# A gated recurrence on one core: groups of three steps of h instead of four, with the products of x made for one pair and for two pairs in turn

## The chip, the cores and the metric

The kernel runs on one core of one Trainium2 chip. The metric is the device time of the whole program in microseconds (us), lower is better. Three runs of the kernel before took 3062.22, 3062.46 and 3062.75 us, so the time before is their median, 3062.46 us.

## The reference

Two layers are computed one after the other on x, which holds 64 sequences of 256 steps of 1024 numbers, all in float32:

```python
xW = jnp.einsum('ntd,dh->nth', x, Wx) + b
def step(prev_h, xw):
    next_h = jnp.tanh(prev_h @ Wh + xw)
    return (next_h, next_h)
...
x = x + h_t
h = jax.nn.silu(q_pool @ W1.T + b1)
gate = jax.nn.sigmoid(h @ W2.T + b2)[:, None, :]
...
a = a * gate
...
return v + a
```

The first layer is a recurrence: h of each step needs h of the step before, times the 1024 x 1024 matrix Wh, plus the row of x Wx of this step, and a tanh. The second layer takes the sequence apart into sums and differences, multiplies every one of them by the same gate of 1024 numbers for each sequence, and puts them together again. Because all are multiplied by one gate, the result is x times (1 + gate); with the residual, x times (2 + gate). The kernel uses that: it makes one `factor` = 2 + gate and multiplies.

## The kernel before, in words

Work comes in **steps** t (0 to 255) and in **pairs** i = t // 2 (0 to 127), since S = 2 steps of x are loaded together as one 512 KB slab. Two kinds of product fill TensorE.

- **A step of h** (`h Wh`, the loop from line 716 on) is done by Strassen's scheme: seven products of blocks instead of eight, each by `strassen_product` (line 192, its matmul is line 197). A product is 16 calls on column strips of 32, and shows in the trace as 32 matmuls and 32 weight loads, so a step is 224 matmuls and 224 weight loads. Between the products ScalarE copies partial sums and does tanh (`tanh`, `put_next`), and VectorE adds, transposes h (`transpose`) and makes the sides of the next step (`strassen_sides`).
- **x Wx of a pair** (class `XWork`, matmul at line 276) is done in three passes of split numbers: `mixed` from x2, then `main` from x1 and from x0, 48 matmuls of 128 x 512 in all (`whole`, line 333). VectorE splits x into `high` (L123), `x2` (`difference`, L305) and `x1` (`low`, L300); ScalarE makes `x0` (`cast`, L311). ScalarE takes `mixed` out of PSUM (`take_mixed`, L321), GpSimd adds the bias (L322), VectorE adds `main` to it (`finish_half`, L376). The tile `sum` then goes to DRAM (`store`, L386) and comes back in another order as the `xw` of two steps (`reload`, L399, eight transfers).

Steps 0 to 11 (up to ALONE = 12) set up the gate and interleave both kinds at a finer grain; the change doesn't touch that part. From step 12 on the order of TensorE, VectorE, ScalarE, GpSimd and SyncE is the order of the program text (`tc.manual_schedule`), so what is written first is queued first on each engine.

In that part the kernel works in **groups** of M = 4 steps of h, and after each group it calls `beside_x(t, mark)`, the **gap**: x Wx of two pairs, named `one` and `two`, while a third (`three`) is split for the next gap. Gaps are at t = 11, 15, ..., 251: 61 of them, and the last has one pair only. PSUM is shared: the banks `main0` and `main1` of x Wx also hold two of the seven products of a step (`m5`, `m7`).

What else a gap does, in program order on SP, the queue that issues the transfers: store `sum` of the pair left from the gap before (held back until the copy `mark` in the last step of the group, by `not_ahead_of`), load x of pair i + 4, reload of the pair just stored, store y of a finished pair, load x of pair i + 5, store and reload of `one`, store y of the second finished pair. GpSimd multiplies the four finished steps by the factor (`scale`, L501). `kept_step` does one of ten early half-finished steps in every second gap (a load, a multiplication on GpSimd, a store). A slab of x is free again once its `store_y` has landed; there are six slabs.

One ScalarE instruction lies inside the group: in its first step, after the first copy, `coming.cast()` makes x0 of the pair that opens the next gap:

```python
if t % M == 0 and coming is not None:
    coming.cast()
```

The tiles `xw` of steps lie in three buffers of a pool; every fourth step (`self.i * S % M + s == M - 1`) uses a fourth buffer, `h0T`.

## Time and profile before

| what | value |
|---|---|
| median of three runs | 3062.46 us |
| the profiled execution's own time | 3049.05 us |
| its span, first to last instruction | 3047.2 us |
| granted TensorE clock, mean | 1.000 |
| matmuls of x Wx (L276) | 4064 + 2032, 389 and 394 ns each |
| matmuls of h Wh (L197), one of its seven groups | 7808 or 8160, 273 ns each |
| VectorE, ScalarE, GpSimd busy | 59%, 28%, 27% of the span |
| transfers of data (queue q1) | 163856 packets, 290.81 MB |
| instruction fetches (queue q8) | 501 packets, 8.21 MB |

The profiled execution took 3049.05 us by its own time, 1.85 us more than its span and 13.4 us less than the median of the runs. The sums of the prediction are made inside the profiled span.

The views are read like this. The timeline lists the instructions of one engine in order of time: start, duration, engine, line, operation, output <- inputs, tile shape, output shape, count; in brackets stands idle time ahead of it. The table of windows gives, for each stretch, its length, then each engine's busy time and count, the granted clock and the share and rate of the DMA engines. The chain of waits follows the last instruction back to what released it. "issue" is time in which an engine waited for nothing that the profile shows.

### The profile page before, as it was taken

To read this page: it belongs to the slowest core of one execution; us is meant where nothing else is said; L and a number is where in the kernel's file an instruction comes from. 1 tells how busy PE (TensorE), PEld (TensorE's weight loads), DVE (VectorE), ACT (ScalarE), POOL (GpSimd) and SP (SyncE) were. 2 spreads that over 40 slices of the span, in tenths; PEclk is the share of its full clock that TensorE was granted. 3 is DMA by queue.
4 is the path that set the end of the run, shared out by engine and by line. 5 is a ranking of instruction groups with operands and counts; after the bars stand their busy time and mean duration, and the time that the engine had idled before them with its cause. 6 is when DMAs were issued, how large, how long until landed. Compare 5 with 4: busy or idle time off the path is not lost.

```text
span 3047.2 us, 141801 instructions
## 1 busy us (share of the span) xinstructions
PE 3029.6 (99%) x63862; PEld 2716.6 (89%) x63862; DVE 1791.4 (59%) x4928; ACT 866.9 (28%) x2641; POOL 808.3 (27%) x521
## 2 busy tenths in 40 slices
PE   9999999999999999999999999999999999999999
PEld 6888898988989989899899898988988989989898
DVE  8555655656656556565565555655656556556565
ACT  3222222322223222222232222222322223222222
POOL 2222222232232231222222222222132222231221
PEclk9999999999999999999999999999999999999999
DMA  7323323233232232322322313223222232232322
GB/s 264 121 83 111 97 88 113 80 104 106 80 120 86 92 119 67 109 88 84 113 77 95 107 65 113 87 85 113 73 99 94 77 113 80 92 112 68 104 92 76
DMA packets 164606, 300.41 MB, mean 99 GB/s; under 512 B 44192, under 2 KB 110496, under 8 KB 164000
## 3 DMA queue, kind: packets, MB, share of 16 engines
q1 hardware_dynamic: 163856, 290.81, 28.2%
q8 instruction: 501, 8.21, 1.1%
q14 instruction: 105, 0.86, 0.1%
q10 hardware_dynamic: 144, 0.52, 0.1%
HBM read 154.93 MB, written 136.31 MB: 96 GB/s over the span
## 4 chain that ended last, share of the span: by engine, by line
PE 99%; issue 0%; POOL 0%; DMA 0%; DVE 0%; SPq 0%; ACT 0%; DVEq 0%
PE main L276 30%; PE acc L197 22%; PE mixed L276 16%; PE m_h L197 14%; PE main_h L197 14%; PE m L197 1%; PE acc L214 0%; PE gate_ps L214 0%; POOL sum L322 0%; DMA wx<-wx 0%; PE acc_raw L214 0%; DVE x L300 0%; SPq L413 0%; ACT sum L321 0%; SPq L119 0%
## 5 line engine op out<-in xcount | busy, mean ns | idle before, releaser
L276 PE MATMUL main<-wx,x 128*128 128x512 f32 x4064 | 945.8, 389 | 0.6 <-DVE x L300 0.6
L276 PEld LDWEIGHTS main<-wx,x 128*128 128x128 f32 x4064 | 762.0, 188 | 161.5 <-issue 2.6
L322 POOL TENSOR_TENSOR sum<-sum,b_row 128x512 f32<-128x512 f32 x254 | 409.9, 1626 | 1119.0 <-ACT sum L321 1109.4
L501 POOL TENSOR_TENSOR x<-x,factor 128x512 f32<-128x512 f32 x242 | 368.2, 1531 | 1007.0 <-issue 561.4
L276 PE MATMUL mixed<-wx,x 128*128 128x512 f32 x2032 | 491.7, 394 | 0.0
L276 PEld LDWEIGHTS mixed<-wx,x 128*128 128x128 f32 x2032 | 376.3, 188 | 89.6 <-issue 12.9
L729 ACT ACTIVATE h<-h 128x128 f32<-128x128 f32 x976 | 275.6, 306 | 568.5 <-DVE h L753 396.7
L300 DVE TENSOR_TENSOR x<-x,x_high 128x1024 fp32r<-128x1024 f32 x127 | 176.9, 1393 | 269.8 <-PE main L276 269.7
L733 DVE STREAM_TRANSPOSE hT<-h 128x128 f32<-128x128 f32 x972 | 297.8, 306 | 38.4 <-ACT h L729 38.3
L376 DVE SCALAR_TENSOR_TENSOR sum<-main,sum 128x512 f32<-128x512 f32 x254 | 175.4, 691 | 203.1 <-PE main L276 181.4
L197 PE MATMUL acc<-wh,s 128*32 128x128 f32 x8160 | 282.6, 273 | 1.3 <-issue 1.0
L197 PE MATMUL acc<-wh,hT 128*32 128x128 f32 x8160 | 279.5, 273 | 1.6 <-issue 1.3
L197 PE MATMUL acc<-t,hT 128*32 128x128 f32 x8160 | 277.8, 273 | 2.2 <-issue 2.0
L197 PE MATMUL m_h<-t,s 128*32 128x128 f32 x7808 | 269.5, 273 | 1.1 <-issue 0.9
L197 PE MATMUL main_h<-wh,s 128*32 128x128 f32 x7808 | 269.7, 273 | 0.8 <-issue 0.6
L197 PE MATMUL main_h<-t,s 128*32 128x128 f32 x7808 | 269.2, 273 | 1.2 <-issue 0.8
L197 PE MATMUL m_h<-wh,hT 128*32 128x128 f32 x7808 | 266.8, 273 | 2.0 <-issue 1.7
L305 DVE SCALAR_TENSOR_TENSOR x<-x_high,x 128x1024 fp32r<-128x1024 f32 x127 | 174.5, 1374 | 155.3 <-PE mixed L276 155.2
L321 ACT ACTIVATE sum<-mixed 128x512 f32<-128x512 f32 x254 | 144.8, 598 | 364.7 <-DMA sum_d<-sum 221.2
L197 PEld LDWEIGHTS acc<-wh,s 128*32 128x32 f32 x8160 | 238.0, 110 | 4.3 <-issue 4.1
L197 PEld LDWEIGHTS m_h<-wh,hT 128*32 128x32 f32 x7808 | 217.8, 110 | 26.3 <-issue 25.9
L614 ACT COPY acc<-xw 128x128 f32<-128x128 f32 x732 | 185.2, 264 | 191.6 <-DVE y L769 102.4
(81 smaller groups left out, 2793.5 us busy)
## 6 DMA issues: line engine op xcount, KB each, us to landing
x<-xT SPq DMA_DIRECT2D x127, 512.0 KB, 4.4
sum_d<-sum SPq DMA_DIRECT2D x127, 512.0 KB, 2.9
xw<-sum_d SPq DMA_DIRECT2D x1016, 64.0 KB, 2.0
yT<-x SPq DMA_DIRECT2D x122, 512.0 KB, 3.5
wh<-wh SPq DMA_DIRECT2D x8, 512.0 KB, 10.7
w<-w1T SPq DMA_DIRECT2D x8, 512.0 KB, 8.6
w<-w2T SPq DMA_DIRECT2D x8, 512.0 KB, 5.0
wx<-wx SPq DMA_DIRECT2D x7, 512.0 KB, 8.6
```

Source lines behind the costliest of these rows:

```text
L197: nc.tensor.matmul(out=out[q * R : (q + 1) * R], lhsT=a[:, k * R : (k + 1) * R], rhs=wh_s.sides[i][k][:, q], start=first and k == 0, stop= ...
L276: nc.tensor.matmul(out=acc[h], lhsT=v[:, k * P : (k + 1) * P], rhs=wx_s[k][which][:, h * HALF : (h + 1) * HALF], start=start and k == 0, s ...
L300: nc.vector.tensor_sub(self.x1, x, self.high)
L305: nc.vector.scalar_tensor_tensor(out=self.x2, in0=self.high, scalar=1.0 + DOWN, in1=pairs[i], op0=ALU.mult, op1=ALU.subtract)
L321: nc.scalar.activation(s, self.mixed[h], AF.Copy, scale=-1.0)
L322: nc.gpsimd.tensor_add(s, s, b_row[:, h * HALF : (h + 1) * HALF])
L376: nc.vector.scalar_tensor_tensor(out=v, in0=self.main[h], scalar=1.0 + DOWN, in1=v, op0=ALU.mult, op1=ALU.add)
L501: nc.gpsimd.tensor_mul(of_step(x, s), of_step(x, s), blocks(factor))
L614: nc.scalar.copy(part, xws[t // S][t % S][:, j])
L729: nc.scalar.activation(quad(h, j), quad(h, j), AF.Tanh)
L733: nc.vector.transpose(quad(hT, j), quad(h, j))
```

## The change

M becomes 3. From step 12 on there are groups of three steps (the last has four), 81 gaps at t = 11, 14, ..., 251, and x Wx of two pairs and of one pair stand in the gaps in turn. `beside_x` gets the pair left over (`later`), the pair that is split (`coming`), the steps to multiply (`scaled`) and the last step of the next group (`end`), and decides by `many` whether it does a second pair. In a gap of one pair the pair's `sum` is not stored at once: it becomes `later`, whose store waits for the `mark` of the next group, as that of `two` did. Loads of x and stores of y are now counted off (`load_next`, `store_done`) instead of being written for fixed pairs; a pair of x is loaded at most five ahead of the last stored one. `kept_step` counts gaps instead of steps. The place of the fourth `xw` buffer is written with 4 instead of M.

```diff
@@ -69,7 +69,7 @@
 E = F // 2
 KB = B // 2
 S = 2
-M = 4
+M = 3
 NP = T // S
 HALF = 512
 HIGH = -(1 << 12)
@@ -390,7 +390,7 @@
             xw = []
             for s in range(S):
                 name = f"xw{self.i * S + s}"
-                if late and self.i * S % M + s == M - 1:
+                if late and (self.i * S + s) % 4 == 3:
 
                     t = const.tile([P, 4, E], F32, tag="h0T", name=name)
                 else:
@@ -629,73 +629,99 @@
     def store_y(i: int) -> None:
         nc.sync.dma_start(out=yT[i], in_=pairs.pop(i))
 
-    def beside_x(t: int, mark):
-
-        i = t // S
-        steps = [(i - 1, 0), (i - 1, 1), (i, 0), (i, 1)] if mark else [(i, 1)]
-        if mark:
+    groups = [M] * ((T - ALONE) // M - 1) + [(T - ALONE) % M + M]
+    done = [ALONE // S - 1]
+    loaded = [i + 3]
+
+    def load_next() -> None:
+
+        k = loaded[0] + 1
+        if k > done[0] + 5:
+            return
+        if k < NP:
+            load_x(k)
+        elif k == NP:
+            ends.append(slab("ends"))
+            nc.sync.dma_start(out=ends[0][:, :W], in_=xN)
+        loaded[0] = k
+
+    def store_done(t: int) -> None:
+
+        while (done[0] + 1) * S <= t + 1:
+            store_y(done[0])
+            done[0] += 1
+
+    def beside_x(t: int, later, coming, scaled: list, end: int, mark):
+
+
+        if later:
             d, dma = later.store()
             not_ahead_of(dma, mark)
-        if i + 4 < NP:
-            load_x(i + 4)
-        if mark:
-            xws[i + 1] = later.reload(d, True)
-        one = coming
-        one.whole()
+        fresh = loaded[0] < NP
+        load_next()
+        if later:
+            xws[later.i] = later.reload(d, True)
+        now, half = coming, len(scaled) // 2
+        many = now.i + 1 < NP and now.i <= end // S
+        now.whole()
         residual(t, hT)
-        for j, r in steps[:2]:
-            scale(pairs[j], r)
-        if mark:
-            store_y(i - 1)
-        if i + 5 < NP:
-            load_x(i + 5)
-        elif i + 4 < NP:
-            ends.append(slab("ends"))
-            nc.sync.dma_start(out=ends[0][:, :W], in_=xN)
-        one.take_mixed()
+        for r in scaled[: half + 1]:
+            scale(pairs[r // S], r % S)
+        if many:
+            store_done(scaled[half])
+            load_next()
+        now.take_mixed()
         if mark:
             accs[:] = [put_part(t + 1, j) for j in range(3)]
-        two = three = None
-        if i + 3 < NP:
-            two = XWork(i + 3)
-            two.difference()
-            two.low()
-        else:
+
+        def prepare():
+            if now.i + 1 == NP:
+                return None
+            nxt = XWork(now.i + 1)
+            nxt.difference()
+            nxt.low()
+            return nxt
+
+        nxt = prepare()
+        if not fresh and not factors:
 
             x_n, factor_n = ends[0][:, :W], ends[0][:, W:]
             nc.vector.transpose(factor_n, factor)
             nc.vector.tensor_mul(x_n, x_n, factor_n)
...
+            factors.append(factor_n)
+        now.finish_half(0)
+        now.finish_half(1)
+        for r in scaled[half + 1 :]:
+            scale(pairs[r // S], r % S)
+        kept_step()
+        if now.i <= end // S:
+            d, _ = now.store()
+            store_done(t)
+            xws[now.i] = now.reload(d, True)
+            if many:
+                now = nxt
+                now.cast()
+                now.whole()
+                now.take_mixed()
+                nxt = prepare()
+                now.finish_half(0)
+                now.finish_half(1)
+                return now, nxt
+            return None, nxt
+        store_done(t)
+        return now, nxt
 
     again = []
 
-    def kept_step(t: int) -> None:
-
-        n, odd = divmod(t // M - ALONE // M, 2)
+    def kept_step() -> None:
+
+        n, odd = divmod(gaps[0], 2)
+        gaps[0] += 1
 
         def at(v, n: int):
             return v[n // S].rearrange("p (b s n) -> p s b n", b=B, s=S)[:, n % S]
 
-        if not 0 <= n <= S * len(kept):
+        if n > S * len(kept):
             return
         if odd and again:
             v = again[0][:].rearrange("p (b g m) -> p g b m", b=B, g=G)
@@ -710,13 +736,14 @@
                 nc.sync.dma_start(out=v, in_=at(kept, n))
 
     accs = [put_part(ALONE, j) for j in range(3)]
-    coming, later, ends = later, None, []
-    coming.cast()
-    later, coming = beside_x(t, None)
+    ends, factors, gaps = [], [], [0]
+    later.cast()
+    later, coming = beside_x(t, None, later, [t], t + groups[0], None)
+    first = ALONE
     for t in range(ALONE, T):
         i, s = divmod(t, S)
         final = t == T - 1
-        last_of_group = t % M == M - 1
+        last_of_group = t == first + groups[0] - 1
         xw = xws[i][s]
         m16, m5, m7 = (bank(tag, f"{tag}_h{t}")[:, :E] for tag in ("m16", "main0", "main1"))
         y = sums.tile([P, 4, E], F32, tag="y", name=f"y{t}")
@@ -745,7 +772,7 @@
 
         strassen_product(m16, sides[1], 1, True)
         nc.scalar.copy(y[:, 0], m16)
-        if t % M == 0 and coming is not None:
+        if t == first and coming is not None:
             coming.cast()
         strassen_product(accs[2], sides[4], 4)
         strassen_product(accs[0], sides[2], 2)
@@ -757,10 +784,10 @@
         if final:
             times_factor(slice(0, E))
             plus_x(slice(0, E))
-        elif t > T - M:
+        elif t > T - 4:
 
             v = x_step(t - 1)
-            nc.vector.tensor_mul(v, v, blocks(factor)) if t < T - 1 else None
+            nc.vector.tensor_mul(v, v, blocks(factor))
             store_y(i - 1) if t == T - S else None
         put_next(0)
         strassen_product(m16, sides[6], 6)
@@ -796,7 +823,10 @@
             nc.vector.tensor_mul(blocks(last[:, :W]), x_step(t), blocks(factor))
             nc.sync.dma_start(out=yT[i][:, :W], in_=last[:, :W])
         elif last_of_group:
-            later, coming = beside_x(t, mark)
+            group = range(first, t + 1)
+            first = t + 1
+            del groups[0]
+            later, coming = beside_x(t, later, coming, list(group), t + groups[0], mark)
         else:
             residual(t, hT)
 
```

## The prediction, made before the change was run

> **What bounds the kernel now.** I read the page first, then who waited for whom on TensorE (PE), then PE's own timeline, cut into steps.

> ```profile
> span 3047.2 us, 141801 instructions
> ...
> PE 3029.6 (99%) x63862; PEld 2716.6 (89%) x63862; DVE 1791.4 (59%) x4928; ACT 866.9 (28%) x2641; POOL 808.3 (27%) x521
> ...
> PE 99%; issue 0%; POOL 0%; DMA 0%; DVE 0%; SPq 0%; ACT 0%; DVEq 0%
> ```

> The chain that ended last is PE alone. So a gain must come from PE's own stream: fewer instructions, or fewer holes between them. The waits of PE show which holes there are:

> ```profile
> PE acc L197 <- issue: 4.3, 11, 0.7
> PE m_h L197 <- issue: 2.6, 8, 0.4
> PE main_h L197 <- issue: 1.5, 5, 0.4
> PE main L276 <- DVE x L300: 0.6, 1, 0.6
> ```

> After the set-up no other engine and no transfer ever makes PE wait; there is only "issue", 8.4 us, all inside products of h. But a slowed stream need not show as idle. So I took from PE's timeline the start of every step and every gap, and measured stretch by stretch. A group without losses (four steps, then the gap), then the worst group, then the last gap, the only one with a single pair:

> ```profile
> core 0: us, PE busy (x), PEclk, DMA share, GB/s
> 2605.84:2611.98 6.14, 6.14 (x226) 1.00 0.02 4
> 2611.98:2618.09 6.11, 6.11 (x233) 1.00 0.02 5
> 2618.09:2624.20 6.11, 6.11 (x232) 1.00 0.02 5
> 2624.20:2630.43 6.23, 6.23 (x233) 1.00 0.09 36
> 2630.43:2652.41 21.98, 21.98 (x100) 1.00 0.54 183
> ...
> 1992.56:1998.69 6.13, 6.13 (x225) 1.00 0.02 5
> 1998.69:2004.81 6.12, 6.12 (x233) 1.00 0.01 4
> 2004.81:2012.25 7.44, 6.61 (x230) 1.00 0.02 4
> 2012.25:2018.93 6.68, 6.62 (x228) 1.00 0.10 36
> ...
> 3005.46:3016.57 11.11, 11.11 (x51) 1.00 0.35 116
> ```

> The first number after a stretch is its length. Full groups take 24.59 us (203.47 to 228.06, and the one above), the worst takes 26.37. Over the 60 full groups I summed what lies above 24.59 us: **28.9 us**, in 41 groups 0.1 us or more. By place: the first two steps lose 0.05 us in all 60 groups together, the third 6.9 us, the fourth 22.0 us. Something that is full at the start of a group runs out in its third or fourth step, and a gap restores it. That is the quantity the change acts on.

> [...] of the 22 holes after 300 us, every one ends 2.3 to 3.0 us after an instruction fetch, so holes come once per block at a fixed place in it. A step has 448 PE instructions (224 matmuls, 224 weight loads), so a lossless step uses a block each 6.115 x 256 / 448 = 3.49 us, while fetches in the group from 1004 us come at 1007, 1011, 1014, 1018, 1022 and 1026, some 3.8 us apart. [...] The trace has it end between 12 and 24 us. [...] h uses strips of 32 columns and x the whole array. [...]

> **Part 1: twenty more gaps.** Gaps at t = 11, 15, ..., 251 are 61; at 11, 14, ..., 251 they are 81. The instructions on PE stay the same: 244 steps, 121 pairs. Each gap costs PE two changes of kind. On the h side: four inner steps of 6.1145 us (7 products of 0.8735) would be 24.46, the lossless group has 24.59, so 0.13. On the x side: two pairs take 21.98, one pair 11.11, so a pair is 10.87 and the gap's fixed cost 0.24. Together 0.37 us, on the path: 20 x 0.37 = **+7.4 us**. Bounds 0.3 and 0.45 us: +6 to +9.

> **Part 2: no fourth step.** 80 of 81 groups end after the third step. The fourth steps' 22.0 us go. The third step's loss is met 80 times, not 60: 6.9 x 80 / 60 = 9.3 us. The last group keeps four steps, before and after. So 28.9 becomes 9.3: **-19.6 us**. The place of block borders in a group wanders in both versions (a group and its gap before are no multiple of 256), so the mean over all groups is the right row; its scatter (0.27 us a group) makes 9.3 into 4 to 18.

> **Part 3: does half a gap refill the reserve?** Counting 256 per fetch and subtracting the PE instructions started, I get the lead of the fetching side up to a constant. It is mostly -20 to -80 late in groups that lost time; of all fetches that fall later than 3.2 us into a gap, in any gap, each finds it at 83 to 106. A short gap is 11.1 us, so I cost this at nothing; without that cover it is the rival below.

> **Part 4: what else lies in a short gap.** VectorE: the end of the step (to 2.0 us after the gap's start), residual 0.7, `high` 0.7, x2 after the mixed pass (1.4), x1 after the x1 pass (1.3), then the two `finish_half`. Of the second pair of a present gap (ending 1051.36):

> ```profile
> 1049.71 0.69 DVE L376 SCALAR_TENSOR_TENSOR sum<-main,sum 128x512 f32<-128x512 f32 x1 [0.64 <-PE main L276]
> 1051.54 0.69 DVE L376 SCALAR_TENSOR_TENSOR sum<-main,sum 128x512 f32<-128x512 f32 x1 [1.14 <-PE main L276]
> 1054.32 0.29 DVE L753 TENSOR_TENSOR h<-acc,y 128x128 f32<-128x128 f32 x1 [2.10 <-PE acc L197]
> ```

> Bank `main0` is free at 1050.4 and `main1` at 1052.2, while `m5` and `m7` first write them 2.6 and 4.4 us after 1051.36: over 3 us of slack, the same in a short gap. ScalarE's `take_mixed` waits for the store of `sum` as now; `put_part` after a short gap takes steps whose xw came a gap earlier, so it waits less. Casts in a first step rise from 61 to 81 at 1.05 us; the first step lost nothing with one in it. GpSimd multiplies two of three steps inside the group, now two of four; 1.5 us each on an engine 27% busy. SP: the same 121 stores and reloads, loads and y stores; a short gap holds one store (2.9 us to land), one load of x, eight reloads (4.6 us to issue) and one y store, some 12 us of queue with `kept_step`; a tail may fall in the first steps of h, where transfers of up to 0.4 MB already lie in several groups without loss. The next store of `sum` waits for `mark` 16 us later. Nothing: 0 us; if this fails by 0.3 us in 40 short gaps, +12.

> **Sum.** -19.6 + 7.4 = -12.2 us of a 3047.2 us span, so 3035.0 there. The runs' median is 13.4 us above the profiled execution's own 3049.05; I take the difference over as it is: 3062.5 - 12.2 = **3050.3 us**, 0.4% faster.

> **Rivals.** (a) *Short gaps refill too little* (slower). For: in the last group, after the only short gap, the third step ended 0.72 us late, six times the mean of 0.12. Against: it is one group, seven of 60 after long gaps lost over 0.5 by there, and the lead above. If 40 groups after short gaps lose 0.72 each: 28.8 + 40 x 0.117 + 7.4 - 28.9 = +12.0, so 3074.5 us. It decides from 0.57 us a group, where the sum passes +6. (b) *The loss is only moved*: supply sets the pace on average, or a wait appears in short gaps, 0.3 us each; -12.2 + 12 = 0, 3062.5 us. For: the lead falls in every group, also without losses. Against: long stretches of PE in gaps use few instructions. (c) *Luck of the block borders is better* and third steps lose half: 4.7 instead of 9.3, so -17, 3045.7 us; counted with the forecast.

> **How the numbers follow.** Forecast with (c): 0.69, from 3043 (loss 4, gaps +6) to 3060 (loss 18, gaps +9). (b) 0.18; (a) 0.13. A measurement of this kernel can tell about 0.2%, 6 us, from no change. Faster, below 3056.4: 0.65 of the forecast and 0.05 of (b), 0.70; same 0.18; slower 0.12. The range leaves out (a) and the far ends: 3043 to 3064.

> **What would show it.** After: span near 3035; groups of three take 18.5 us, losing about 0.12 on average, all in the third step; gaps 11.1 and 22.0 us in turn; PE "issue" well under 8 us. Wrong if groups after short gaps lose more than those after long ones (rival a), or if PE waits for another engine at the start of a group (b).

## The result and the profile after

The changed kernel took 3055.27 us, median of 15 runs (3049.82 to 3056.55); the kernel before took 3062.22 us beside it, median of 15 (3054.38 to 3066.93). The ratio is 0.9976 with a 95% interval of 0.9968 to 0.9984: 7 us or 0.24% faster, where I had forecast 12.2 us. The time lies in the range that was given; but that range, 3043 to 3064 us, also held the time of no change at all, so the interval of the ratio, which leaves out 1, says more.

The profiles seem to say the opposite. The profiled execution of the kernel before had taken 3049.05 us, less than any of the 15 runs; the one after took 3056.46 us by its own time, among the highest of its runs. The page of after begins:

```profile
span 3054.6 us, 141755 instructions
...
PE 3039.8 (100%) x63862; PEld 2716.7 (89%) x63862; DVE 1796.3 (59%) x4928; ACT 864.0 (28%) x2641; POOL 772.3 (25%) x521
...
PE 99%; issue 0%; POOL 0%; DMA 0%; DVE 0%; SPq 0%; ACT 0%; DVEq 0%
```

The number of matmuls is the same and PE still bounds all; its busy time rose by 10 us because a stretch in which matmuls come late counts mostly as busy: of the last two steps of the worst group below, 6.89 and 8.14 us long, 6.58 and 6.83 us count so, against 6.12 and 6.22 in the group without loss. So the two pages can't be subtracted: they are executions in which the same stream ran at different speeds. The waits of PE after (in total, times, longest):

```profile
PE acc L197 <- issue: 4.0, 9, 0.7
PE main_h L197 <- issue: 2.1, 7, 0.3
PE m_h L197 <- issue: 0.6, 2, 0.3
PE main L276 <- DVE x L300: 0.4, 1, 0.4
```

"issue" is 6.7 us, against 8.4 before. No wait for another engine came in its place: the 0.4 us for VectorE lie in the set-up. The table of windows of after, PE alone (stretch, its length, PE's busy time and count, granted clock, DMA share and GB/s): a group of three without loss, a long gap, a group that lost 0.35 us, a short gap, and the worst group.

```profile
core 0: us, PE busy (x), PEclk, DMA share, GB/s
1858.48:1864.62 6.14, 6.14 (x225) 1.00 0.01 3
1864.62:1870.74 6.12, 6.12 (x233) 1.00 0.02 5
1870.74:1876.96 6.22, 6.22 (x232) 1.00 0.10 35
1876.96:1898.94 21.98, 21.98 (x100) 1.00 0.55 184
1898.94:1917.77 18.83, 18.83 (x673) 1.00 0.05 15
1917.77:1928.88 11.11, 11.11 (x50) 1.00 0.51 170
1928.88:1935.02 6.14, 6.14 (x226) 1.00 0.03 7
1935.02:1941.91 6.89, 6.58 (x231) 1.00 0.02 4
1941.91:1950.05 8.14, 6.83 (x234) 1.00 0.21 68
```

Gaps are 22.0 and 11.1 us in turn and a lossless group takes 18.48 us (three steps of 6.1145 and 0.13 at the end), as the prediction had it. But the 80 groups of three lose 28.0 us together in this execution, 0.35 us each, where I had put 0.12.

In what follows, the **loss** of a group is its length, from its first matmul of h to the first matmul of the gap, less 6.1145 us a step and 0.132 us. It is taken from the start of each matmul in the trace, over all full groups but the last, which ends with the program. A **set** is what was timed side by side on one chip; the four sets of experiments ran on four different chips. A run with one time only is the profiled execution itself.

### The profile page after: what moved, and what is told of

Read it like the earlier page. It is cut to its first block, busy times and chain, and to the rows that moved or that the text cites. A ratio compares the mean times of both kernels' runs of the same rounds, so it can differ in the third digit from the quotient of the medians.

```text
span 3054.6 us, 141755 instructions
## 1 busy us (share of the span) xinstructions
PE 3039.8 (100%) x63862; PEld 2716.7 (89%) x63862; DVE 1796.3 (59%) x4928; ACT 864.0 (28%) x2641; POOL 772.3 (25%) x521
## 4 chain that ended last, share of the span: by engine, by line
PE 99%; issue 0%; POOL 0%; DMA 0%; DVE 0%; SPq 0%; ACT 0%; DVEq 0%
PE main L276 30%; PE acc L197 22%; PE mixed L276 16%; PE m_h L197 14%; PE main_h L197 14%; PE m L197 1%; PE acc L214 0%; PE gate_ps L214 0%; POOL sum L322 0%; DMA wx<-wx 0%; PE acc_raw L214 0%; DVE x L300 0%; SPq L413 0%; ACT sum L321 0%; SPq L119 0%
## 5 line engine op out<-in xcount | busy, mean ns | idle before, releaser
L276 PE MATMUL main<-wx,x 128*128 128x512 f32 x4064 | 945.7, 389 | 0.4 <-DVE x L300 0.4
L276 PEld LDWEIGHTS main<-wx,x 128*128 128x128 f32 x4064 | 762.1, 188 | 161.2 <-issue 2.2
L501 POOL TENSOR_TENSOR x<-x,factor 128x512 f32<-128x512 f32 x242 | 312.0, 1289 | 1318.3 <-DVE x L619 931.5
L322 POOL TENSOR_TENSOR sum<-sum,b_row 128x512 f32<-128x512 f32 x254 | 421.0, 1667 | 849.0 <-ACT sum L321 840.5
L276 PE MATMUL mixed<-wx,x 128*128 128x512 f32 x2032 | 494.7, 395 | 0.0
L276 PEld LDWEIGHTS mixed<-wx,x 128*128 128x128 f32 x2032 | 374.9, 188 | 92.8 <-issue 17.1
L300 DVE TENSOR_TENSOR x<-x,x_high 128x1024 fp32r<-128x1024 f32 x127 | 178.7, 1407 | 265.5 <-PE main L276 265.5
L376 DVE SCALAR_TENSOR_TENSOR sum<-main,sum 128x512 f32<-128x512 f32 x254 | 175.4, 691 | 205.2 <-PE main L276 179.8
L197 PE MATMUL acc<-wh,s 128*32 128x128 f32 x8160 | 283.7, 273 | 2.7 <-issue 2.4
L197 PE MATMUL acc<-wh,hT 128*32 128x128 f32 x8160 | 277.8, 273 | 0.7 <-issue 0.6
L197 PE MATMUL acc<-t,hT 128*32 128x128 f32 x8160 | 276.0, 273 | 1.0 <-issue 0.9
L197 PE MATMUL main_h<-wh,s 128*32 128x128 f32 x7808 | 269.9, 273 | 1.3 <-issue 1.1
L197 PE MATMUL main_h<-t,s 128*32 128x128 f32 x7808 | 269.9, 273 | 1.2 <-issue 0.9
L197 PE MATMUL m_h<-t,s 128*32 128x128 f32 x7808 | 269.7, 273 | 0.8 <-issue 0.6
L197 PE MATMUL m_h<-wh,hT 128*32 128x128 f32 x7808 | 263.7, 274 | 0.2
L197 PEld LDWEIGHTS acc<-wh,s 128*32 128x32 f32 x8160 | 237.5, 110 | 7.0 <-issue 7.0
L197 PEld LDWEIGHTS m_h<-wh,hT 128*32 128x32 f32 x7808 | 213.8, 110 | 30.1 <-issue 29.5
L197 PEld LDWEIGHTS acc<-wh,hT 128*32 128x32 f32 x8160 | 234.0, 110 | 3.7 <-issue 2.6
```

Of the source, the lines that this page charges most:

```text
L197: nc.tensor.matmul(out=out[q * R : (q + 1) * R], lhsT=a[:, k * R : (k + 1) * R], rhs=wh_s.sides[i][k][:, q], start=first and k == 0, stop= ...
L276: nc.tensor.matmul(out=acc[h], lhsT=v[:, k * P : (k + 1) * P], rhs=wx_s[k][which][:, h * HALF : (h + 1) * HALF], start=start and k == 0, s ...
L300: nc.vector.tensor_sub(self.x1, x, self.high)
L322: nc.gpsimd.tensor_add(s, s, b_row[:, h * HALF : (h + 1) * HALF])
L376: nc.vector.scalar_tensor_tensor(out=v, in0=self.main[h], scalar=1.0 + DOWN, in1=v, op0=ALU.mult, op1=ALU.add)
L501: nc.gpsimd.tensor_mul(of_step(x, s), of_step(x, s), blocks(factor))
```

## The experiments

**Both kernels again, on one chip.** No edit.

> The kernel before, unchanged, for a second profile. If the loss of a group follows how long the instruction fetches take in the execution at hand, the loss over its 60 full groups lies near 42 us here, because the median of the runs is 13 us above the first profile, which lost 28.9 us; its third steps then lose more than 0.12 us each, near 0.2, and the first two steps still nothing. If the loss is a fixed property of the program, it is 29 us again, with 0.12 us in the third step.

> The changed kernel, unchanged, for a second profile on the same chip as the kernel before. Loss by fetching: groups after short and after long gaps lose the same within their scatter, some 0.3 us each, all in the third step. Rival, short gaps refill too little: groups after short gaps lose at least twice as much as those after long ones, and lose it from the second step on.

The first lines of the two pages, before and then after:

```profile
span 3046.6 us, 141801 instructions
```

```profile
span 3039.9 us, 141755 instructions
```

Times: 3048.48 and 3041.75 us, one run each; the kernel before had a median of 3046.51 us in this set. The loss before was 28.9 us again, some 0.12 us of each group's 0.48 by the end of the third step: so my guess of 42 us was wrong for this set, whose median was not 3062 us either; those first runs were not profiled. The changed kernel lost 13.8 us, in 40 groups after long gaps 0.181 us each and in 40 after short gaps 0.164 us, all but 0.01 of it in the third step. So half a gap refills as well as a whole one here.

**Groups of two.** Only short gaps, 121 of them.

```diff
-M = 3
+M = 2
-    groups = [M] * ((T - ALONE) // M - 1) + [(T - ALONE) % M + M]
+    groups = [M] * ((T - ALONE) // M - 2) + [2 * M]
```

> Groups of two steps with one pair in every gap, 121 gaps, the last group of four steps. Loss by fetching: two steps end before the reserve does, so the groups lose under 0.05 us each, and the 60 further gaps cost 0.37 us each: 22 - 42 + 4 = -16 us against the kernel before, near 3046 us. Rival, short gaps refill too little: with short gaps alone the second step loses 0.3 us or more, and the time is above the kernel before, 3062 + 22 + 36 - 42 = 3078 us. Rival, the loss is only moved (the mean rate of supply decides): the same total loss in 121 groups, 3062 + 22 = 3084 us.

3045.59 us, ratio 0.9998 (0.9990 to 1.0006). Windows of PE, two lossless groups with their gaps:

```profile
1110.53:1116.66 6.13, 6.13 (x225) 1.00 0.02 4
1116.66:1122.89 6.23, 6.23 (x232) 1.00 0.10 37
1122.89:1133.99 11.10, 11.10 (x52) 1.00 0.51 172
1133.99:1140.13 6.14, 6.14 (x225) 1.00 0.01 3
1140.13:1146.36 6.23, 6.23 (x233) 1.00 0.10 36
1146.36:1157.46 11.10, 11.10 (x52) 1.00 0.52 173
```

The 120 groups lose 6.7 us in all, 0.056 each, so both rivals fall: behind short gaps alone the loss is small, and it is not merely moved. The loss fell by 22.2 us against the kernel before, and the 60 further gaps took 13.1 us in the gaps and 60 x 0.132 = 7.9 us at the group ends. It comes out even, where I had expected 16 us less, because there were 29 us to win, not the 42 I had put in.

**A pause without a gap.** In the kernel before, after the second step of each group:

```diff
+        if t % M == 2:
+            spare = bank("mixed0", f"spare{t}")
+            for q in range(Q):
+                nc.tensor.matmul(
+                    out=spare[q * R : (q + 1) * R],
+                    lhsT=sides[1][:, :R],
+                    rhs=wh_raw[0][:, :HALF],
+                    start=True,
+                    stop=True,
+                    skip_group_check=True,
+                    tile_position=(0, q * R),
+                )
```

> The kernel before with four more matmuls of 512 columns on column strips after the second step of each group, into a bank that is free there and whose content nobody reads: 16 instructions that keep TensorE busy some 0.87 us, 53 us in all, and no change of tiling. Loss by fetching: in that stretch the fetching side runs ahead again by most of what two steps cost it, so the fourth step loses less than half of what it loses in the kernel before (under 0.2 us a group), and the time is some 35 to 45 us over the kernel before instead of 53. If the loss came from other engines' results or from the fourth step's own place in the group, it stays at its 0.4 to 0.6 us and the time is 53 us over.

3078.61 us in one run, 32 us over the median of before; I had expected 35 to 45. PE's timeline at such a pause (start, duration, operation, output <- inputs, shapes, count), then the window of the two steps behind it:

```profile
690.72 1.06 PE L197 MATMUL acc<-wh,s 128*32 128x128 f32 x32
691.60 1.04 PE L749 MATMUL spare<-wh,hT 128*32 128x512 f32 x8
692.46 0.40 PE L197 MATMUL m_h<-wh,hT 128*32 128x128 f32 x8
```

```profile
692.46:704.83 12.37, 12.37 (x453) 1.00 0.07 23
```

The pause costs 0.867 us; behind it the third and fourth steps take 12.37 us, two lossless steps and the end of the group. Over the 60 groups the loss apart from the pauses is 0.066 us each, against 0.48. The tiling and the third and fourth steps are the same, so the fourth step's place in the group is not the cause, and a stretch in which PE is busy but uses few instructions (16 in 0.867 us, where h at 13.65 ns each uses 64) mends the loss. By itself the pause also gives the other engines 0.87 us to catch up; the run with more instructions, below, speaks against that reading. As a remedy the pause is too dear.

**Strips for x Wx: an edit without effect.** A switch for strips was added to the function that issues the matmul of x Wx, and no caller set it:

```diff
-    def x_matmul(acc, v, which: int, h: int, k: int, start=False, stop=False) -> None:
+    def x_matmul(acc, v, which: int, h: int, k: int, start=False, stop=False, strips=False) -> None:
...
+        for q in range(Q if strips else 1):
```

> The changed kernel, with every matmul of x Wx in the gaps (128 columns wide) issued as four matmuls on strips of 32 columns, the tiling that the steps of h use, with the same numbers. It tests the price of a gap. If the 0.37 us come from the change of tiling and four strips run side by side as they do in h, a gap of one pair goes from 11.11 to 10.9 us or less and the end of a group loses its 0.13 us: 81 x 0.37 = 30 us less than the changed kernel, some 37 us under the kernel before; the fetching side still refills, since a strip pair takes 384 instructions in 10.9 us, half of what h takes. If the four strips don't run side by side with four-byte single-pass operands, x Wx of 121 pairs takes up to four times 10.87 us and the time is thousands of us over. If the price of a gap has another cause (a wait that the profile doesn't show), gaps stay at 11.1 and 22.0 us and the time is that of the changed kernel or, with the refill spoiled, 10 to 20 us over it.

> Groups of two steps and one pair in every gap, with x Wx on strips. If both the price of a gap and the loss by fetching are as I hold, neither is left: 121 gaps at about nothing instead of 61 at 0.37 us (-22 us) and under 8 us of loss instead of 29 (-21 us): some 40 us under the kernel before. If strips don't run side by side, thousands of us over; if they spoil the refill of the reserve, the second step of each group loses 0.3 us or more and it ends near or over the kernel before.

The groups of instructions show that nothing went out on strips (the shape is 128*128 and the count as before):

```profile
L278 PE MATMUL main<-wx,x 128*128 128x512 f32 x4064 | 945.8, 389 | 0.2 <-DVE x L303 0.2
```

So these two say nothing on strips, and whether x Wx on strips would save the price of a gap was not tried; that the price, 0.37 us, comes from the change of tiling, as the expectations suppose, stays unshown. Of strips the traces show that the 32 matmuls of a product of h, 273 ns each by the page, overlap within 0.8735 us, and that the pause's eight of 128x512 took 0.867 us, 0.108 us each, where those of x Wx on the whole array take 10.87 / 48 = 0.226 us. The two runs stand as further measurements of the changed kernel and of groups of two in a set where the kernel before took 3041.68 us: the changed kernel 3040.06 us, ratio 0.9993 (0.9987 to 1.0000), loss 13.4 us; groups of two 3044.92 us, 1.0008 (1.0002 to 1.0015), loss 6.3 us.

**Transfers beside h.** In the kernel before:

```diff
-            not_ahead_of(dma, mark)
```

> The kernel before without the wait that holds the store of the left-over pair's sum back until the last step of the group, so that this store and the next load of x (1 MB) go out at the start of the group, while h is computed. If transfers of data slow the instruction fetches, fetches that meet them take longer (over 1.3 us instead of 1.0), the reserve ends earlier and a group loses 0.6 us or more instead of 0.48. If fetch times don't depend on the data traffic, the loss stays at 0.4 to 0.55 us a group and the time within 5 us of the kernel before.

3128.68 us in one run, 87 us over the median of before in its set. Windows of two first steps of a group that met as many transfers, one that lost 0.94 us and one that lost nothing (all engines; the last two numbers are DMA share and GB/s):

```profile
core 0: us, PE busy (x) PEld busy (x) DVE busy (x) ACT busy (x) POOL busy (x), PEclk, DMA share, GB/s
738.84:745.92 7.08, 6.34 (x224) 6.08 (x227) 2.96 (x10) 2.76 (x8) 0.00 (x0) 1.00 0.51 171
888.39:894.53 6.14, 6.14 (x226) 6.14 (x229) 2.61 (x9) 2.52 (x8) 0.00 (x0) 1.00 0.54 191
```

The loss is 108 us, 1.81 us a group, and begins in the first step (0.16 us on average). The waits of PE there are again "issue", 50 us of it, and in the steps of h 0.7 us for other engines. But my explanation by longer fetches is not borne out: the mean fetch took 1.07 us, as in the kernel before (1.09). The supply of instructions is late all the same. In the steps of h of this run 200 matmuls start more than 0.15 us after the one before them, and every one of them starts 2.2 to 3.2 us after an instruction fetch began (in the kernel before 66 do, all 2.2 to 3.0 us after one), though under a quarter of all matmuls of h start in that stretch. The spacing of fetches grew instead: after a fetch of up to 0.95 us the next came 3.67 us later on average, against 3.58 in the second profile of before. So transfers do slow the supply of a dense stream of PE, not every time; why, with each fetch as short as before, stays open.

**Both kernels once more.** No edit.

> The kernel before, unchanged, for a profile on the same chip as the next run, so that the loss of both can be set against their times. Loss by fetching: its groups' losses and the changed kernel's, with 7.3 us for the twenty more gaps, add up to the difference of the two spans within 1 us. If something else moves, they don't.

> The changed kernel, unchanged, timed again and profiled beside the run before this one. If the gain is the loss taken away less a fixed price, its ratio follows the loss that the chip at hand shows: with 29 us lost before, 15 us less loss and 7.3 us of gaps, about -7 us (0.9976); with 24 us lost before, -2 to -4 us (0.999).

Before 3044.85 us, changed 3040.98 us, ratio 0.9986 (0.9978 to 0.9995). Spans 3043.5 and 3043.3 us; losses of the full groups 26.5 and 17.1 us, gaps and group ends +7.2 us: -2.2 us, where the spans differ by -0.2. So the sum of full groups misses by 2.0 us, not within the 1 us expected. The rest is the last group, which has four steps in both kernels and was 1.8 us longer in the changed one. Its first two steps, before and then after (DMA share and GB/s last):

```profile
3013.32:3019.45 6.13, 6.13 (x225) 1.00 0.49 187
3019.45:3025.66 6.21, 6.21 (x232) 1.00 0.28 77
```

```profile
3011.34:3017.47 6.13, 6.13 (x225) 1.00 0.66 253
3017.47:3025.00 7.53, 6.62 (x232) 1.00 0.26 79
```

This is not chance. In all four profiles of the changed kernel the second step of the last group took 7.4 to 7.6 us, in the three of the kernel before 6.1 to 6.4. There 1.5 to 1.6 MB of transfers begin in the first step, against 1.1 MB before, and the second fetch of the group comes 4.9 to 5.1 us after the first, against 3.8. It looks like the case of the transfers beside h; no run took them away.

**More instructions.** In the kernel before, after each of the seven products of a step, one tiny matmul:

```diff
+            nc.tensor.matmul(
+                out=spare[:R, :8],
+                lhsT=sides[1][:, :R],
+                rhs=wh_raw[0][:, :8],
...
+                tile_position=(0, 0),
+            )
```

> The kernel before with one tiny matmul (8 columns, one strip, four instructions) after each of the seven products of a step of h from step 12 on, into a bank that is free there and that nobody reads: 28 more instructions in a step's 448. What they cost by themselves shows in the first step of a group, where the reserve covers. Loss by fetching: each step now takes 6% more from the reserve, so it ends about a step earlier, and the later steps of a group grow by some 0.3 to 0.4 us more than the first: a loss of 1.2 to 1.8 us a group above the tiny matmuls' own cost, instead of 0.48, with loss already in the second step. If the loss has another cause, every step grows by the same and the loss stays near 0.5 us a group.

A miss. A step grew from 6.14 to 6.52 us already in the first of a group: 0.385 us for 28 instructions, 13.75 ns each, the pace at which h uses them anyway (6.115 us / 448 = 13.65 ns). So the stream was not made denser. The steps took 6.52, 6.56, 6.59 and 6.97 us on average where their shortest were 6.52, 6.56, 6.52 and 6.82. Against the shortest of its kind a group loses some 0.2 us; against the growth of its first step, as the expectation has it, 0.5 us, half of the difference being 0.15 us that every last product has more, even the shortest. Neither is the 1.2 to 1.8 us I had forecast, and why it is not more than before stays open. One thing it does tell: here the other engines had 1.5 us more in every group, without fewer instructions on PE, and 0.2 to 0.5 us of loss stayed, where the pause with 0.87 us and 16 instructions left 0.066.

**The store of `sum` two products later.** The groups of three lose on average 0.08 us up to the start of their last product and 0.09 more from there to the gap; this asks for the cause of the second part. In both kernels:

```diff
-        mark = nc.scalar.copy(u, m16)
+        nc.scalar.copy(u, m16)
...
-        tanh(1)
+        mark = tanh(1)
```

> The changed kernel with the store of the left-over pair held back until the last tanh of the group instead of the copy two products earlier, so that the last product of a group runs without transfers beside it. In the profiles of the changed kernel a group of three loses 0.08 us on average up to the start of its last product and 0.09 more in that product and at the change to x Wx, where before a third step in mid-group loses 0.02 there. If the transfers that begin two products ahead of the end cause it, the loss after the start of the last product falls to 0.03 us: 80 x 0.06 = 5 us less than the changed kernel, near 0.997 of the kernel before. If it is the change to x Wx itself that finds the reserve low, it stays at 0.07 to 0.10 and the time is that of the changed kernel within 1.5 us.

> The kernel before with the same later store. Its groups lose 0.31 to 0.38 us up to the start of their last product and 0.11 to 0.13 more after it. If the transfers cause the latter, it falls to some 0.05 and the time by 60 x 0.07 = 4 us, to 0.9987; if the change to x Wx does, the time is the same within 1.5 us.

In this set the kernel before, without the edit, took 3039.46 us; the changed kernel without it was not run there. Changed kernel with it: 3039.39 us, ratio to the kernel before 1.0000 (0.9992 to 1.0008). Kernel before with it: 3041.66 us, 1.0009 (1.0000 to 1.0017). The edit did move the transfers: in the last product none begin now, where 210 to 240 KB did. The loss behind the start of the last product stays: 0.12 and 0.06 us after long and short gaps, and 0.11 in the groups of four. So the transfers are not its cause. It goes with how many steps the reserve has had to cover instead, which is a comparison of runs and not an experiment of its own: 0.024 us in groups of two and 0.026 with the pause, 0.09 in groups of three, 0.11 in groups of four.

## Why the prediction was right, and where its sizes were off

| run | step 1 | step 2 | step 3 | step 4 | loss a group, us |
|---|---|---|---|---|---|
| before, second profile | 38 | 10 | -14 | -26 | 0.48 |
| before with the pause after step 2 | 37 | 12 | 20 | -3 | 0.07 |
| changed, second profile | 32 | 11 | -14 | | 0.17 |
| groups of two | 27 | 8 | | | 0.06 |
| before, transfers not held back | -21 | -29 | -33 | -48 | 1.81 |
| before with more instructions | 34 | 15 | -1 | -9 | 0.2 to 0.5 |

The lead falls from the first step to the second while PE still runs at full pace, so it is the supply that lags and not PE that holds the fetches up. The pause lifts the lead and takes the loss away; the transfers lower it from the first step on and bring more loss. In the second profile of before, a block of 256 instructions whose fetch took up to 0.95 us was followed by the next fetch after 3.6 us on average, one whose fetch took 1.25 to 1.5 us after 3.9 us, while PE uses a block in 3.49 us. So the pace of supply goes with the length of each fetch; that is a correlation (0.5 to 0.6 in three profiles), not an experiment, and the transfers show that it is not the whole of it.

**Part 1, twenty more gaps: right.** Between the two profiles of one set, the gaps take 4.5 us more (1330.6 to 1335.1 us) and the 20 more group ends 20 x 0.132 = 2.6 us: 7.1 us, against 7.4. The groups of two bear it out. Where the price comes from was not tested.

**Part 2, no fourth step: right in kind, too large in size.** I wrote "The fourth steps' 22.0 us go" and let 9.3 us remain. 13.8, 13.4 and 17.1 us remained in three sets, 28.0 us in the first. The mis-sized term is the third step at the end of a group. Of the fourth step's loss, 0.11 us a group, 6.4 us in all, lay behind the start of its last product, where PE changes to x Wx, and belongs to whichever step stands last. A third step in mid-group loses 0.026 us there, a third step at the end 0.087: 80 x 0.061 = 4.9 us more than in my sum, and 9.3 + 4.9 = 14.2 is close to the 13.8 of that set. In the first profile of the changed kernel this explains only a part: 12 of its 28.0 us lie behind the start of the last product, and the third steps had lost about as much before it. Why the supply was slower in that execution is not known. The 0.13 us I had taken for a group's end came from groups without loss, with the reserve still there; the ends cost more where the lead is low.

**Part 3, half a gap is enough: right.** Groups of two lose 0.056 us behind short gaps alone. Over four profiles of the changed kernel the groups behind short gaps lose 0.25 us and those behind long ones 0.20, with a scatter of 0.3 us a group: a difference up to 0.1 us is not excluded. The late last group of before that I had held against it was chance: by the end of its third step it was 0.2 and 0.1 us late in the two later profiles.

**Part 4, nothing else in the way: right but for transfers in a first step.** PE waits for no other engine after the set-up. That transfers in the first steps cost nothing was too broad: without the wait for `mark` the groups lost 80 us more. In the changed kernel itself the last group, where more transfers lie beside the first step, was 1.4 to 1.9 us longer than before in each pair of profiles; the prediction had put it at nothing.

**The sum.** In the set with both second profiles the change gives 13.8 - 28.9 + 7.1 = -8.0 us in the full groups and +1.9 us in the last; the set-up was 0.6 us shorter, and the spans differ by -6.7 us. Between the two first profiles the same terms are 28.0 - 28.9 + 7.4 = +6.5, +1.4 and -0.5 us, and the spans differ by +7.4. So the terms are complete; what is not known beforehand is the loss of an execution. The ratios are 0.9976, 0.9993 and 0.9986 in sets where before took 3062, 3042 and 3045 us, as a gain would that is a share of the loss less a fixed price; three sets don't prove it. If the first set's before lost 42 us, 28.0 - 42 + 7.4 + 1.4 = -5 us of its -7; but that loss was not profiled.

**Where it was luck.** I had called anything above 3056.4 us, 6 us under before, the same. The first set, with 7 us, came out on the right side of that mark; the two later sets, with 1.6 and 3.9 us, would not have. So the direction and the mechanism hold, but the forecast of 12.2 us was nearly twice the best of three sets and more than three times the middle one.

## What to carry to other kernels

When PE alone bounds a kernel and its waits show only "issue", cut its timeline into equal pieces of work and compare each with the shortest of its kind: the profile called 8 us idle where 29 us were lost, since late matmuls counted mostly as busy here (6.83 us of a step of 8.14). If the loss grows with the distance from the last stretch of wide matmuls, as it did here from 0.05 us in the first two steps of all groups to 22.0 us in the fourth, ask whether it is a supply of instructions that runs short: count what has been fetched less what has been started, and put in a pause that uses few instructions. If it is, put such stretches closer together, but price each change between the two kinds of work by a group whose reserve is low, not by a lossless one: the third step lost 0.087 us behind the start of its last product at a group's end, 0.026 in mid-group. Take a loss of this sort from several executions before building a sum on it.

## What the runs showed of the hardware

- At 13.65 ns an instruction, PE's stream of column-strip matmuls outran its supply in these runs: after some two steps (900 instructions) stalls came, mostly 0.2 to 0.7 us each, and they ended 2.2 to 3.2 us after an instruction fetch began (66 of 66 late matmuls within 3.0 us in the kernel before, 200 of 200 within 3.2 without the wait for `mark`).
- 16 instructions that keep PE busy for 0.87 us gave back enough for two further steps: the loss of a group fell from 0.48 to 0.07 us.
- The same program lost 26 to 29 us in three executions in this way, and the changed one 13 to 28 in four; the medians of the kernel before lay between 3039 and 3062 us in five sets.
- Transfers of some 2.7 MB laid beside a group of four steps (1.1 MB of it in the first) cost 1.3 us a group, with fetches no longer than before but further apart.
